# Turning the exponentials of an attention block with VectorE and DMA in place of TensorE

## The chip, the cores and the metric

The kernel runs on one core of a Trainium2 chip. The metric is the device time of one execution in microseconds. Before the change three runs took 4974.77, 4978.38 and 4980.49 us; the median is 4978.38 us.

## The reference

Four images of 32 x 32 tokens with 768 channels pass through two layers. Each layer normalizes its input by groups of channels, applies multi-head attention over the 1024 tokens of an image with relative-position biases, projects the result and adds the input again:

```python
qkv = x @ Wqkv                                    # 12 heads of 64 channels
rel_h = jnp.einsum('bhwc,hkc->bhwk', r_q, Rh)     # position biases made from q
rel_w = jnp.einsum('bhwc,wkc->bhwk', r_q, Rw)
scores = scale * q @ k.T + rel_h[..., :, None] + rel_w[..., None, :]
attn = jax.nn.softmax(scores, axis=-1)
out = (attn @ v) @ Wproj + bproj
x = x + out
```

The second layer scales q once more and adds a bias to q, k and v. Everything is in 32-bit floats.

## The kernel before

The kernel holds channels on partitions and tokens along a row. There are eight images in all (two layers of four), and each image has six pairs of heads, so 48 pairs. A pair's 1024 queries are cut into eight tiles of 128; the program calls (pair g, tile n) a unit, and a loop goes over 384 units. Units 0 to 3 of a pair are its first half of queries, units 4 to 7 the second.

What happens to a unit:

- `biases` (line 283): GpSimd adds the two position biases into an `sc` tile of 128 queries x 1024 keys, one for each of the two heads.
- `scores` (L295 to L313): TensorE multiplies q by k into a PSUM tile of two banks. VectorE adds the bias and finds the minimum of the negated sum in one instruction (L302), ACT takes the exponential with its sum (L306), VectorE inverts the sum (L310), and GpSimd scales the row (L313). The result is in `sc`, with queries on partitions.
- `transposes` (L328 to L333): the product with v needs keys on partitions. TensorE turns the 128 x 1024 tile of each head in eight blocks of 128 x 128, four to a PSUM tile `tr`. ACT copies the first four into `pt` (L331), VectorE the other four (L333). `pt` holds one half of the queries, 512, for all 1024 keys, and each head has one buffer of it.
- `weigh` (L343): after four units TensorE multiplies `pt` by v, 16 products for the two heads, which the profile counts as 32 matmuls. VectorE copies the result to `attn` (L347).

Beside this run the projections of the next pair. `project_in` (L207) makes q, k and v in groups of six products into PSUM tiles of the pool `ps_m`; `positions` (L250 to L273) makes the position products from q, copies them to a tile `t` (ACT, L255), stores them in DRAM (`tdr`, L258) and loads them back in a skewed order as `rel`, with 16 transfers of 32 partitions x 8 pieces of 128 bytes for each pair (L273). `turn_values` (L235) turns v with TensorE. `project_out` (L363, L369, L370) makes the output of the image that has ended: twelve groups, each of which loads the residual `res` (L360), adds it on VectorE and stores the sum. They are spread over the first two pairs of the next image. `load_x` and `norm_stats` fetch and measure the next image near the end of pair 4, and `norm_apply` normalizes it at the start of pair 5.

The order of TensorE's instructions is the program's own (`manual_schedule`). In each unit it is: the scores of the next unit, some groups of projections (`take`), a weighing that is due, the transposes of this unit, and turned values. The instructions of the other engines are ordered by a list scheduler, which takes whatever is ready in its own model, the earliest in the program first; once made, each engine's order is fixed, and an instruction that has to wait holds all that come behind it on its engine. All transfers are issued from SP's queue.

A half's weighing is done one unit after the half's last transposes: in unit 4 for the first half, and in unit 0 of the next pair for the second.

PSUM has eight banks: two score tiles of two banks (`ps_s`), two tiles of one bank for transposes (`ps_t`), and two for products (`ps_m`).

Of the kernel before, what the change touches and what calls it, by code (L numbers as in the profile page):

```python
# [42 lines left out]
def attention_blocks(ctx: ExitStack, tc: tile.TileContext, a: dict, out: bass.AP):  # L45
# [3 lines left out]
    const = ctx.enter_context(tc.tile_pool(name="const", bufs=1))  # L49
    wpool = ctx.enter_context(tc.tile_pool(name="weights", bufs=2))  # L50
    xpool = ctx.enter_context(tc.tile_pool(name="x", bufs=10))
    apool = ctx.enter_context(tc.tile_pool(name="attn", bufs=8))
    qkpool = ctx.enter_context(tc.tile_pool(name="qk", bufs=2))
    vtpool = ctx.enter_context(tc.tile_pool(name="vt", bufs=1))
    vpool = ctx.enter_context(tc.tile_pool(name="v", bufs=2))
    scpool = ctx.enter_context(tc.tile_pool(name="sc", bufs=6))
    ptpool = ctx.enter_context(tc.tile_pool(name="pt", bufs=2))
    tpool = ctx.enter_context(tc.tile_pool(name="t", bufs=1))
    relpool = ctx.enter_context(tc.tile_pool(name="rel", bufs=2))
    iopool = ctx.enter_context(tc.tile_pool(name="io", bufs=4))  # L60
    small = ctx.enter_context(tc.tile_pool(name="small", bufs=4))
    dram = ctx.enter_context(tc.tile_pool(name="scratch", bufs=1, space=bass.MemoryType.DRAM))
    dram2 = ctx.enter_context(tc.tile_pool(name="scratch2", bufs=2, space=bass.MemoryType.DRAM))
    ps_s = ctx.enter_context(tc.tile_pool(name="ps_s", bufs=2, space=PSUM))
    ps_t = ctx.enter_context(tc.tile_pool(name="ps_t", bufs=2, space=PSUM))
    ps_m = ctx.enter_context(tc.tile_pool(name="ps_m", bufs=2, space=PSUM))
# [17 lines left out]
    def load_w(g):  # L84
        im, pair = divmod(g, NP)
        w = wpool.tile([P, NC, 3 * P], FP, tag="w", name=f"w_{g}")
        w_of[g] = w
        nc.sync.dma_start(out=w, in_=a[f"wqkv{images[im][0]}"][pair].rearrange("p (c o) -> p c o", c=NC))

# [63 lines left out]
    def group_mean(cols, name):  # L153
        t = ps_t.tile([P, HALF], FP, tag="t", name=f"gm_{name}")
        for c in range(NC):
            nc.tensor.matmul(
                t[0:NG, 0:1], lhsT=grp[:, c, :], rhs=cols(c), start=(c == 0), stop=(c == NC - 1)
            )
        return t[0:NG, 0:1]

    def to_channels(g, name):
        t = ps_t.tile([P, HALF], FP, tag="t", name=f"gb_{name}")
        for c in range(NC):
            nc.tensor.matmul(  # L164
                t[:, c : c + 1], lhsT=grpT[:, c * P : (c + 1) * P], rhs=g, start=True, stop=True
            )
        return t[:, 0:NC]
# [27 lines left out]
    def project_in(g, which, i):  # L195

        im, pair = divmod(g, NP)
        l = images[im][0]
        xn, w = xn_of[im], w_of[g]
        cols = slice(i * HALF, (i + 1) * HALF)  # L200
        if i == 0:
            pool = vtpool if which == 2 else qkpool
            qkv_of[g, which] = pool.tile([P, S], FP, tag="qkv"[which], name=f"{'qkv'[which]}_{g}")
        to = qkv_of[g, which]
        t = ps_m.tile([P, HALF], FP, tag="m", name=f"pj_{g}_{which}_{i}")
        for c in range(NC):
            nc.tensor.matmul(  # L207
                t, lhsT=w[:, c, which * P : (which + 1) * P], rhs=xn[c][:, cols],
                start=(c == 0), stop=(c == NC - 1),
            )  # L210
            if c < NC - 1:
                yield True
# [16 lines left out]
    def turn_values(g, i):  # L229
        if i == 0:  # L230
            v_of[g] = vpool.tile([P, NT, P], FP, tag="v", name=f"v_{g}")
        t = ps_t.tile([P, 4, P], FP, tag="t", name=f"vt_{g}_{i}")
        for j in range(4):
# [4 lines left out]
    def positions(g, i):  # L238
# [7 lines left out]
        for j in range(4):  # L246
            for h in range(2):
# [5 lines left out]
                )  # L253
        t = tpool.tile([P, 2, 4, P], FP, tag="t", name=f"t_{g}_{i}")
        nc.scalar.copy(t, ps)  # L255
# [19 lines left out]

    sc_of, sps_of, pt_of, attn_of = {}, {}, {}, {}

# [36 lines left out]

    def transposes(g, n):
        half, j = divmod(n, 4)
        for h in range(2):
            if j == 0:
                pt_of[g, half, h] = ptpool.tile(
                    [P, NT, HALF], FP, tag=f"pt{h}", name=f"pt_{g}_{half}_{h}", bufs=1  # L320
                )
            pt = pt_of[g, half, h]
            sc = sc_of[g, n, h].rearrange("p y x -> p (y x)")
            for i in range(2):
                t = ps_t.tile([P, 4, P], FP, tag="t", name=f"tr_{g}_{n}_{h}_{i}")
                for k in range(4):
                    at = 4 * i + k
                    nc.tensor.transpose(t[:, k, :], sc[:, at * P : (at + 1) * P], ident)  # L328
                to = pt[:, 4 * i : 4 * i + 4, j * P : (j + 1) * P]
                if i == 0:  # L330
                    nc.scalar.copy(to, t)  # L331
                else:
                    nc.vector.tensor_copy(to, t)  # L333

    def weigh(g, half):
        im, pair = divmod(g, NP)
        if half == 0:
            attn_of[g] = apool.tile([P, S], FP, tag="attn", name=f"attn_{g}")
        av = ps_m.tile([P, HALF], FP, tag="m", name=f"av_{g}_{half}")
        for k in range(NT):  # L340
            for h in range(2):
                rows = slice(h * D, (h + 1) * D)
                nc.tensor.matmul(  # L343
                    av[rows, :], lhsT=v_of[g][:, k, rows], rhs=pt_of[g, half, h][:, k, :],
                    start=(k == 0), stop=(k == NT - 1),
                )
        nc.vector.tensor_copy(attn_of[g][:, half * HALF : (half + 1) * HALF], av)  # L347

    def project_out(im, o, i):
# [3 lines left out]
        if i == 0:  # L353
            wo_of[im, o] = wpool.tile([P, NC, P], FP, tag="wo", name=f"wo_{im}_{o}")
            nc.sync.dma_start(
                out=wo_of[im, o], in_=a[f"wo{l}"][o].rearrange("p (c o) -> p c o", c=NC)
            )
# [38 lines left out]
    with tc.manual_schedule(engines={mybir.EngineType.PE}):  # L396
# [13 lines left out]
        outs, todo = [], []  # L410
        pending = None
        for at, (g, n) in enumerate(units):
            im, pair = divmod(g, NP)
            last = pair == NP - 1
            if n == 0 and g + 1 < NPAIR:
                todo = prepare(g + 1)
            if outs and n == 1:
                todo = (
                    todo[:-4] + outs[0:2] + todo[-4:-2] + outs[2:4] + todo[-2:] + outs[4:6]
                )  # L420
                outs = outs[6:]
            if n == 6 and pair == NP - 2 and im + 1 < NI:
                load_x(im + 1)
# [8 lines left out]
            if at + 2 < len(units):  # L432
                biases(*units[at + 2])
            turn = list(late)
            late.clear()
            if not last or n > 1:
                take(todo, -(-6 * len(todo) // (NT - n)))
            if pending:
                weigh(*pending)
                if pending[1] == 1 and (pending[0] + 1) % NP == 0:  # L440
                    outs = put_out(im - 1 if pair == 0 else im)
                pending = None
            transposes(g, n)
            run(turn)
            if n == NT - 1:
                take(todo, 6 * len(todo))
                run(early)
                run(late)
            if n % 4 == 3:
                pending = (g, n // 4)  # L450
        weigh(*pending)
        outs = put_out(NI - 1)
# [48 lines left out]
```

## Time and profile before

| What | Value |
| --- | --- |
| Median of three runs | 4978.38 us |
| Profiled execution, its own time | 4976.71 us |
| Its span, first to last instruction | 4974.8 us |
| TensorE (PE) busy | 4631.3 us, 93% |
| VectorE (DVE) busy | 1874.0 us, 38% |
| ACT busy | 1587.2 us, 32% |
| GpSimd (POOL) busy | 2303.6 us, 46% |
| TensorE clock granted, mean | 0.971 |
| DMA: packets, bytes, share of 16 engines on SP's queue | 359664, 226.68 MB, 15.3% |

The page gives busy times by engine, the chain of work that ended last (followed back from the last instruction, at each step to what released it), and groups of instructions by line. In a line of a group, the name before `<-` is what is written and the names after it are what is read; then come the shape, the count, the busy time, the mean nanoseconds of one, and the idle time of the engine before them with what ended it. A chain cut to a stretch of time gives the shares of the lines in that stretch. SP's lines show the start, the length and the count of a row of DMA issues. The DMA share is the mean busy share of the 16 DMA engines.

### The profile page before, as it was taken

The page shows a single profiled execution, that of the slowest core. Times are in us where ns is not written, and L with a number is a line of the kernel's source. Part 1 is how long each engine was busy: PE and PEld are TensorE (multiplying, and loading weights), DVE is VectorE, ACT ScalarE, POOL GpSimd, SP SyncE. Part 2 cuts the span into 40 slices and gives each one's busy share as a digit, 9 for nine tenths or more (in the row PEclk, how much of TensorE's full clock was granted, in tenths as well). Part 3 has the DMA queues.
Part 4 walks back from the last instruction along what each step waited for, and adds up shares of the span by engine and source line. Part 5 has one row for each costly group of instructions (what it writes and reads, how often), then busy time and mean ns, then how long its engine had stood idle before and what let it go on. Part 6 is the DMA issues. An engine that isn't in the chain of part 4 may idle for free.

```text
span 4974.8 us, 50961 instructions
## 1 busy us (share of the span) xinstructions
PE 4631.3 (93%) x19200; PEld 2242.9 (45%) x19200; DVE 1874.0 (38%) x3328; ACT 1587.2 (32%) x2616; POOL 2303.6 (46%) x1555
## 2 busy tenths in 40 slices
PE   8999899999999999999999999999999999999998
PEld 4444444444444444444444444444444444444444
DVE  3434433334333443334433343333433334333342
ACT  2333322333223332233322333223332233322331
POOL 3555433554335543355433554335543455433552
PEclk9999999999999999999999999999999999999999
DMA  3111111111111111111011110111101111011101
GB/s 112 32 33 35 48 58 57 33 31 52 58 57 34 40 42 58 58 35 54 26 57 58 35 58 23 57 58 36 58 23 57 58 35 41 23 57 62 31 13 55
DMA packets 359908, 229.94 MB, mean 46 GB/s; under 512 B 218352, under 2 KB 316656, under 8 KB 353520
## 3 DMA queue, kind: packets, MB, share of 16 engines
q1 hardware_dynamic: 359664, 226.68, 15.3%
q8 instruction: 153, 2.51, 0.2%
q14 instruction: 91, 0.75, 0.0%
HBM read 151.10 MB, written 75.50 MB: 46 GB/s over the span
## 4 chain that ended last, share of the span: by engine, by line
PE 86%; ACT 9%; issue 3%; DMA 2%; DVE 1%; POOL 0%; SPq 0%; ACTq 0%; POOLq 0%; DVEq 0%
PE pj L207 31%; PE s L295 16%; PE av L343 14%; PE tr L328 11%; PE o L363 11%; ACT pt L331 5%; ACT t L255 2%; PE tp L250 2%; ACT sc L306 1%; PE vt L235 1%; DMA tdr<-t 1%; PE gb_rstd L164 0%; DMA xn<-in_x 0%; DVE st L150 0%; PE gb_mean L164 0%
## 5 line engine op out<-in xcount | busy, mean ns | idle before, releaser
L283 POOL TENSOR_TENSOR sc<-rel 128x1024 f32<-128x1024 f32 x768 | 1452.0, 1909 | 1069.0 <-PE tr L328 979.6
L207 PE MATMUL pj<-xn,w 128*128 128x512 f32 x3456 | 1567.1, 602 | 1.1 <-DVE xn L187 1.1
L313 POOL TENSOR_SCALAR sc<-sc,sm 128x1024 f32<-128x1024 f32 x768 | 849.5, 1118 | 1516.0 <-DVE sm L310 1509.0
L306 ACT ACTIVATE sc<-sc,sm 128x1024 f32<-128x1024 f32 x768 | 879.6, 1146 | 1140.7 <-DVE sm L302 1140.7
L302 DVE CUSTOM_DVE_ANT_0 sc<-s,sc 128x1024 f32<-128x1024 f32 x768 | 911.1, 1222 | 781.7 <-PE s L295 720.4
L207 PEld LDWEIGHTS pj<-xn,w 128*128 128x128 f32 x3456 | 634.8, 190 | 909.3 <-issue 902.6
L328 PE MATMUL tr<-ident,sc 128*128 128x128 f32 x6144 | 841.8, 281 | 211.6 <-ACT pt L331 208.1
L331 ACT COPY pt<-tr 128x512 f32<-128x512 f32 x768 | 448.3, 584 | 1761.5 <-PE tr L328 1760.0
L295 PE MATMUL s<-k,q 64*128 64x512 f32 x3072 | 900.1, 649 | 70.1 <-ACT t L255 68.6
L328 PEld LDWEIGHTS tr<-ident,sc 128*128 128x128 f32 x6144 | 683.9, 142 | 548.6 <-issue 363.5
L333 DVE COPY pt<-tr 128x512 f32<-128x512 f32 x768 | 530.1, 690 | 722.7 <-PE tr L328 717.1
L343 PE MATMUL av<-pt,v 128*64 128x512 f32 x3072 | 685.8, 599 | 0.0
L363 PE MATMUL o<-attn,wo 128*128 128x512 f32 x1152 | 534.8, 617 | 0.0
L295 PEld LDWEIGHTS s<-k,q 64*128 64x128 f32 x3072 | 304.3, 196 | 392.5 <-issue 251.7
L343 PEld LDWEIGHTS av<-pt,v 128*64 128x64 f32 x3072 | 215.3, 138 | 463.4 <-issue 441.5
L363 PEld LDWEIGHTS o<-attn,wo 128*128 128x128 f32 x1152 | 222.4, 197 | 314.3 <-issue 314.3
L347 DVE COPY attn<-av 128x512 f32<-128x512 f32 x96 | 66.4, 691 | 720.9 <-PE av L343 720.9
L310 DVE RECIPROCAL sm<-sm 128x2 f32<-128x2 f32 x384 | 63.2, 165 | 402.2 <-ACT sc L306 402.2
L369 DVE SCALAR_TENSOR_TENSOR res<-o,bo,res 128x512 f32<-128x512 f32 x96 | 72.0, 750 | 237.1 <-PE o L363 232.7
L306 ACT ACTIVATION_READ_ACCUMULATOR sc<-sc,sm 128x1 f32 x768 | 143.2, 186 | 0.0
L255 ACT COPY t<-tp 128x1024 f32<-128x1024 f32 x96 | 97.2, 1012 | 132.2 <-PE tp L250 83.6
L250 PE MATMUL tp<-tab,q 64*128 64x128 f32 x1536 | 107.8, 283 | 1.4 <-issue 0.7
(47 smaller groups left out, 772.2 us busy)
## 6 DMA issues: line engine op xcount, KB each, us to landing
w<-in_wqkv SPq DMA_DIRECT2D x48, 1152.0 KB, 5.1
tdr<-t SPq DMA_DIRECT2D x192, 256.0 KB, 2.8
rel<-tdr SPq DMA_DIRECT2D x768, 32.0 KB, 2.0
wo<-in_wo SPq DMA_DIRECT2D x48, 384.0 KB, 3.2
xn<-in_x SPq DMA_DIRECT2D x24, 512.0 KB, 6.3
res<-in_x SPq DMA_DIRECT2D x48, 256.0 KB, 2.7
mid<-res SPq DMA_DIRECT2D x48, 256.0 KB, 2.1
xn<-mid SPq DMA_DIRECT2D x24, 512.0 KB, 6.6
```

The lines of the kernel that those rows point to most:

```text
L207: nc.tensor.matmul(t, lhsT=w[:, c, which * P : (which + 1) * P], rhs=xn[c][:, cols], start=(c == 0), stop=(c == NC - 1),)
L250: nc.tensor.matmul(ps[:, h, j, :], lhsT=q[rows, at * P : (at + 1) * P], rhs=tabs[l][rows, :], start=True, stop=True,)
L283: nc.gpsimd.tensor_tensor(sc, rel[:, h, 0, n, :].unsqueeze(2).to_broadcast([P, HW, HW]), rel[:, h, 1, n, :].unsqueeze(1).to_broadcast([P, ...
L295: nc.tensor.matmul(ps[h][:, cols], lhsT=q[rows, n * P : (n + 1) * P], rhs=k[rows, cols], start=True, stop=True,)
L302: nc.vector.tensor_tensor_reduce(out=sc, in0=ps[h], in1=sc, scale=-1.0, scalar=BIG, op0=ALU.add, op1=ALU.min, accum_out=st[:, 0, h : h + 1],)
L306: nc.scalar.activation(sc, sc, AF.Exp, bias=st[:, 0, h : h + 1], scale=-1.0, accum_out=st[:, 1, h : h + 1],)
L313: nc.gpsimd.tensor_scalar(sc, sc, st[:, 2, h : h + 1], 1.0, ALU.mult, ALU.mult)
L328: nc.tensor.transpose(t[:, k, :], sc[:, at * P : (at + 1) * P], ident)
L331: nc.scalar.copy(to, t)
L333: nc.vector.tensor_copy(to, t)
L343: nc.tensor.matmul(av[rows, :], lhsT=v_of[g][:, k, rows], rhs=pt_of[g, half, h][:, k, :], start=(k == 0), stop=(k == NT - 1),)
L363: nc.tensor.matmul(t, lhsT=w[:, c, :], rhs=attn_of[im * NP + c][:, cols], start=(c == 0), stop=(c == NC - 1),)
```

## The change

The turning by TensorE goes, with the PSUM pool `ps_t` and the copies on ACT and VectorE. In its place:

- VectorE turns each head's 128 x 1024 tile in blocks of 32 x 32, one instruction for each tile and head, into a tile `tb`. Two units share one `tb`. After this a block's keys lie on the 32 partitions that held its queries, so they are not yet on the partitions of their keys.
- After every second unit SP issues 16 transfers for each head, from SBUF to SBUF. Each moves, from 32 partitions of `tb` to 32 partitions of `pt`, eight pieces of 64 floats (256 bytes) on each partition.
- `pt` holds queries in another order (quarter, block, unit, query); the copy to `attn` is made in two parts that restore it.
- The weighing of a half moves one unit later, to units 5 and 1, behind the start of the next half's turning.
- There are three score tiles in PSUM. The turned values and the small products of the normalization use the pool `ps_m`.
- Buffers in SBUF: `x` tiles 7 instead of 10, residuals (`io`) 2 instead of 4, `attn` 7 instead of 8. The projected v and the tile `t` of positions, which had buffers of their own, share the six of `sc`. The weights of a pair come as three tiles (q, k, v) of 384 KB with four buffers, instead of one of 1152 KB with two.
- The twelve output groups of an image are spread over units 2 to 7 of the next image's first pair and, from unit 0, over its second.

```diff
-    xpool = ctx.enter_context(tc.tile_pool(name="x", bufs=10))
-    apool = ctx.enter_context(tc.tile_pool(name="attn", bufs=8))
+    xpool = ctx.enter_context(tc.tile_pool(name="x", bufs=7))
+    apool = ctx.enter_context(tc.tile_pool(name="attn", bufs=7))
...
-    iopool = ctx.enter_context(tc.tile_pool(name="io", bufs=4))
+    tbpool = ctx.enter_context(tc.tile_pool(name="tb", bufs=4))
+    ptpool = ctx.enter_context(tc.tile_pool(name="pt", bufs=1))
+    iopool = ctx.enter_context(tc.tile_pool(name="io", bufs=2))
...
-    ps_s = ctx.enter_context(tc.tile_pool(name="ps_s", bufs=2, space=PSUM))
-    ps_t = ctx.enter_context(tc.tile_pool(name="ps_t", bufs=2, space=PSUM))
+    ps_s = ctx.enter_context(tc.tile_pool(name="ps_s", bufs=3, space=PSUM))
...
+    def turn(g, n):
+        half, quarter, j = n // 4, n // 2 % 2, n % 2
         for h in range(2):
+            if n % 4 == 0:
+                pt_of[g, half, h] = ptpool.tile(
+                    [P, NT, 2, 4, 2 * HW], FP, tag=f"pt{h}", name=f"pt_{g}_{half}_{h}"
+                )
             if j == 0:
-                to = pt[:, 4 * i : 4 * i + 4, j * P : (j + 1) * P]
-                if i == 0:
-                    nc.scalar.copy(to, t)
-                else:
-                    nc.vector.tensor_copy(to, t)
+                tb_of[h] = tbpool.tile([P, HW, 2, HW], FP, tag="tb", name=f"tb_{g}_{n}_{h}")
+            tb, pt = tb_of[h], pt_of[g, half, h]
+            nc.vector.transpose(tb[:, :, j, :], sc_of[g, n, h])
+            if j == 1:
+                for y in range(4):
+                    for r in range(4):
+                        nc.sync.dma_start(
+                            out=pt[32 * y : 32 * y + 32, :, quarter, r, :],
+                            in_=tb[32 * r : 32 * r + 32, y::4, :, :].rearrange("p k n i -> p k (n i)"),
+                        )
...
-            if pending:
-                weigh(*pending)
...
-            transposes(g, n)
-            run(turn)
+            if n % 4 == 1 and at > 4:
+                weigh(*(units[at - 2][0], n // 4 ^ 1))
+                if n == 1 and pair == 0:
+                    outs = put_out(im - 1)
+            run(ready)
```

In the new loop `turn(g, n)` stands ahead of the projections of the unit.

## The prediction

> **What bounds the kernel now.** I read the page's shares first, then the chain that ended last, then the chain over single stages, then the groups, and last SP's queue, which the change loads. The chain by engine and by line:
>
> ```profile
> PE 86%; ACT 9%; issue 3%; DMA 2%; DVE 1%; POOL 0%; SPq 0%; ACTq 0%; POOLq 0%; DVEq 0%
> PE pj L207 31%; PE s L295 16%; PE av L343 14%; PE tr L328 11%; PE o L363 11%; ACT pt L331 5%; ACT t L255 2%; PE tp L250 2%; ACT sc L306 1%; PE vt L235 1%; DMA tdr<-t 1%; PE gb_rstd L164 0%; DMA xn<-in_x 0%; DVE st L150 0%; PE gb_mean L164 0%
> ```
>
> TensorE is the bound. The transposes hold it directly (tr, 11%) and a second time through the copy that it waits for (pt, 5%). One unit of the chain in order of time (start, duration, what) shows how:
>
> ```profile
> 2778.76 1.92 PE s L295 x8
> 2780.67 3.63 PE pj L207 x8
> 2784.30 0.45 PE tr L328 x4
> 2784.76 0.02 issue
> 2784.78 0.59 ACT pt L331
> 2785.37 0.14 issue
> 2785.51 1.11 PE tr L328 x8
> 2786.62 1.92 PE s L295 x8
> ```
>
> From 2784.30 to 2786.62, 2.3 us of each unit, TensorE serves the turning of the exponentials. The groups that the change removes, and the row by which I price its new VectorE work:
>
> ```profile
> L302 DVE CUSTOM_DVE_ANT_0 sc<-s,sc 128x1024 f32<-128x1024 f32 x768 | 911.1, 1222 | 781.7 <-PE s L295 720.4
> L328 PE MATMUL tr<-ident,sc 128*128 128x128 f32 x6144 | 841.8, 281 | 211.6 <-ACT pt L331 208.1
> L331 ACT COPY pt<-tr 128x512 f32<-128x512 f32 x768 | 448.3, 584 | 1761.5 <-PE tr L328 1760.0
> L333 DVE COPY pt<-tr 128x512 f32<-128x512 f32 x768 | 530.1, 690 | 722.7 <-PE tr L328 717.1
> ```
>
> Stages differ, so I cut one image (2475.9 to 3093.7 us, 617.8 us) at its weighings. The chain by line of a pair with output projections (2475.9 to 2598.8), then of the two halves of a pair without (2721.7 to 2769.2 and 2769.2 to 2811.7):
>
> ```profile
> by line: PE o L363 26.8%; PE pj L207 26.1%; PE s L295 14.0%; PE av L343 11.4%; PE tr L328 9.6%; ACT pt L331 4.8%; DMA tdr<-t 2.3%; ACT t L255 1.7%; issue 1.4%; PE vt L235 1.1%; PE tp L250 0.9%; SPq L258 0.3%; ACTq L255 0.0%; ACTq L331 0.0%
> ...
> by line: PE pj L207 40.5%; PE s L295 16.4%; PE av L343 14.8%; PE tr L328 13.4%; ACT pt L331 5.0%; PE tp L250 4.7%; ACT t L255 4.3%; issue 1.7%; ACTq L255 0.1%; ACTq L331 0.0%
> ...
> by line: PE pj L207 32.7%; PE s L295 18.8%; PE av L343 16.5%; PE tr L328 14.7%; ACT pt L331 6.7%; issue 4.4%; PE vt L235 3.8%; ACT sc L306 2.9%; DVE sc L302 0.2%; DVE sm L302 0.2%; ACTq L331 0.0%; DVEq L302 0.0%
> ```
>
> **What comes off TensorE.** Without tr, pt, their issue time, the wait for the copy of t and the landing of tdr, the pair with outputs falls from 122.9 to about 98.6 us (9.6, 4.8, 1.7, 2.3 and 1.4% taken off). The halves without outputs fall from 47.5 to 35.9 us (13.4, 5.0, 4.3 and 1.7% off) and from 42.5 to 32.5 us (14.7 and 6.7% off, and 1 us of issue). I take the waits for t as gone: t gets one of six buffers in place of one, and with three score tiles in PSUM a score no longer needs the tile that ACT is copying. If both stay, the pair costs 2 to 5 us more.
>
> **What is added, and where it queues.** VectorE gets 768 block transposes of 128x1024. The trace has none. From below, the nearest 1024-column row is the normalization at L187 (808 ns); from above, twice L302 (2.44 us); I take L302's 1.22 us, f32 at the same width. 768 x 1.22 = 937 us against 530 us of copies removed: VectorE goes from 1874 to about 2290 us, half of any likely span. The attention copy in two halves of 256 columns adds some 10 us of its 66. None of it is on the path while VectorE is half idle; at 2.44 us it would be near 3230 us, still under the span, but the last transposes of a half would come later. ACT loses 448 us.
>
> SP gets 48 pairs x 4 x 2 x 16 = 6144 transfers of 32 partitions x 8 pieces of 256 bytes (64 KB). Nothing in the trace moves SBUF to SBUF. The nearest row is rel<-tdr, also 32 partitions x 8 pieces, in bursts of 16; first SP's queue, then the page's row with the time to landing:
>
> ```profile
> 990.58 8.94 SPq L273 DMA_DIRECT2D rel<-tdr  x16
> ...
> 1082.72 7.84 SPq L273 DMA_DIRECT2D rel<-tdr  x16
> ```
>
> ```profile
> rel<-tdr SPq DMA_DIRECT2D x768, 32.0 KB, 2.0
> ```
>
> Many bursts take 7.72 us: 0.48 us for each transfer, 0.56 in the dear bursts. A lone load or store issues in 0.33 us; xn loads go at 0.68 (three in 2.04). Ends 0.33 and 0.68; I take 0.48, that of the same shape. 6144 x 0.48 = 2960 us of SP: it fits the span in total. The DMA engines are at 15%; while a rel burst runs their share is 0.37 to 0.48, so pieces of twice the bytes make at most 0.96, still under the rate of issue, but narrowly. So the cost is not a sum but a loop.
>
> **The loop.** Each head has one pt buffer. The first 32 transfers of a half (issued from unit 1 or 5) overwrite what the weighing in that same unit reads, so they start when it ends; 32 more follow (unit 3 or 7); the next weighing needs the last landing. From weighing end to last landing: 64 x 0.4825 = 30.9 us, plus 1.5 us (2.0 to landing less the last issue) = 32.4. The weighing takes 7.0 (32 matmuls, 7.02 us in the chain). The loop is 39.4 us a half, whatever TensorE does. The first half also has four tdr (median 0.38) and two w issues (0.36) in SP's queue, with some 0.04 us between instructions: 2.4 us; the second has one w, 0.4. The sixteen rel issues, 7.7 us, I put at nothing: they wait for tdr's landing, so they come behind the second 32, while SP has 8.5 us of landing and weighing with no pt transfer to issue. If they come in front, each first half pays 7.7.
>
> TensorE's own halves, 35.9 and 32.5 us, are shorter than the loop, so it idles before the weighing: 39.4 + 2.4 - 35.9 = 5.9 us, and 39.8 - 32.5 = 7.3. What such a pause costs next, by stage (us, busy and count of each engine, granted clock, DMA share, GB/s):
>
> ```profile
> 3120.00:3124.00 4.00, 0.75 (x4) 0.32 (x4) 0.00 (x0) 1.01 (x1) 0.00 (x0) 0.88 0.42 131
> 3124.00:3128.00 4.00, 4.00 (x7) 1.35 (x6) 1.62 (x3) 0.82 (x1) 0.00 (x0) 0.50 0.47 135
> 3128.00:3132.00 4.00, 4.00 (x8) 1.62 (x7) 1.66 (x4) 1.67 (x4) 0.46 (x1) 0.77 0.38 59
> ```
>
> After a pause of 3.25 us TensorE works about 6 us at a granted clock of one half, which loses some 2.9 us, and here the weighing itself runs in it. Halves: 39.4 + 2.4 + 2.9 = 44.7 and 39.4 + 0.4 + 2.9 = 42.7, a pair 87.4 us where 90.0 were. Nearly all that TensorE gains there goes to the loop. The Trainium skill ("TensorE: Matmul & The Clock Gate", Part 1: The HAM clock gate) has the same sign: half rate after an idle window of about 3.4 us.
>
> A rule of the skill speaks against the change: "DMA: Bandwidth & Descriptors", Rules for kernel authors, wants small transfers coalesced, since under 64 KB one pays mostly overhead; its table gives 0.95 us for 64 KB. Were these serial, a half would be an estimated 64 x 0.95 + 9 = 70 us and the kernel near 6900. The rel bursts, each landing 2.0 us after an issue 0.48 us behind the last, overlap, so the row decides.
>
> **Smaller buffers.** x tiles go from 10 to 7: five tiles of the next image instead of two are loaded only when the old ones are released, at the end of pair 4, in SP's queue behind up to 15 us of pt issues, and the normalization waits for all. That half had 50.1 us with a 4.87 us wait on xn. Bounds: 43.7 (as before, turning gone) to 65 (15 us of queue, cold clock); I take 55. The residual's buffers go from 4 to 2: a load waits for the landing of the store two before it, behind a burst of 15 us. VectorE is in order, so a late residual holds it, and with it the scores and the evacuations. Outputs come about 13 us apart (one in each of the four units of a 52 us half), so two of them cover most: 0 to 20 us a pair, taken as 4, and 1.4 where the loop shows.
>
> **Sum.** An image: two pairs with outputs at 104, two at 87.4, pair 4 at 44.7 + 55, pair 5 at 87.7: 570 us against 617.8, less 47.6, seven times: 333. The first image, without outputs, gains about 20; the last weighing now waits for 32 issues and a landing, about 20 lost. The profiled execution (span 4974.8, time 4976.7, 1.7 under the median of 4978.4) falls to a span of 4642, so about 4645.
>
> **Rivals.** (1) The transfers are hidden. At 0.33 us a half's loop is 64 x 0.33 + 1.5 + 7.0 = 29.6, under TensorE's halves. Then only the tr, pt and t chains go: about 490 us an image, 4050 in all. For: lone issues take 0.33. Against: every issue in a row took more. (2) rel comes in front of the second 32, or SP blocks on a transfer whose wait ends later: 7.7 to 10 us on the first half of pairs 2 to 5, 31 to 40 an image, 4860 to 4940. For: rel now goes out 13 us after the first tdr (1069.27 to 1082.72), which could fall ahead of the second 32. Against: those need only VectorE, ready earlier. (3) Slower: issue of the new transfers. The gain of 333 us is spread over about 8 loop-bound halves an image; 5 us a half takes it back, 0.08 us a transfer: from 0.56 us on, the dear rel burst, the kernel is not faster. At 0.68 the loop is 43.5 + 8.5 = 52 us, 55 with the clock, in all twelve halves: about 680 an image, 5450. For: two 256-byte sides on 32 partitions, unmeasured. Against: rel's 0.48, in the same shape.
>
> **How the numbers follow.** Forecast 0.50 (4500 to 4800), hidden 0.12, queue 0.13, slower issue 0.25. Of the forecast, 0.01 falls within 0.2% of 4978 (10 us, about what a measurement tells from no change) and 0.02 above; of the queue case 0.02 and 0.02. Faster 0.47 + 0.12 + 0.09 = 0.68, same 0.03, slower 0.25 + 0.04 = 0.29. The range goes from 4350, half way to hidden, to 5150, an issue of about 0.60; about 0.1 is left out at each end. The likeliest case's own range is 4500 to 4800.
>
> **What would show it.** No tr or pt copies; pt<-tb x6144 on SP at 0.48 us, landing 2 us; VectorE's transposes at 1.2 us; av waiting for DMA some 6 us in pairs 2 to 5, not in pairs 0 and 1; clock below 0.97. It is wrong if the issue period is another, if av starts without waiting, or if TensorE waits longer at the norms or outputs than I gave.

## The result, and the profile after the change

The changed kernel takes 6078.85 us (median of four runs, 6076.74 to 6082.63) against 4977.52 us before: a ratio of 1.2213, with an interval of 1.2192 to 1.2234. It is 22% slower where the forecast said 7% faster. The profiled execution took 6077.1 us, its span is 6075.4 us, and TensorE's mean granted clock fell from 0.971 to 0.814.

The busy times on the page, and the chain that ended last by engine and by line:

```profile
PE 4051.5 (67%) x13056; PEld 1654.8 (27%) x13056; DVE 2266.8 (37%) x3424; ACT 1141.9 (19%) x1848; POOL 2301.8 (38%) x1555
...
SPq 30%; PE 22%; DMA 5%; issue 3%; DVE 2%; POOL 1%; ACT 1%; DVEq 0%; ACTq 0%
SPq L338 27%; PE av L350 8%; PE pj L210 5%; PE o L376 4%; PE s L298 3%; SPq L276 3%; DMA pt<-tb 2%; DMA tdr<-t 2%; DVE tb L334 1%; PE tp L253 1%; DMA xn<-mid 1%; ACT sc L309 1%; DMA res<-mid 0%; POOL sc L286 0%; SPq L261 0%
```

SP's queue was at 0% of the chain and is now its largest part, nearly all of it L338, the new transfers. TensorE, 93% busy before, is at 67%. (The followed chain accounts for some two thirds of the span; the rest is not attributed.) The groups that wait for the transfers:

```profile
L350 PE MATMUL av<-pt,v 128*64 128x512 f32 x3072 | 982.2, 734 | 1583.2 <-DMA pt<-tb 1470.7
...
L334 DVE STREAM_TRANSPOSE tb<-sc 128x1024 f32<-128x1024 f32 x768 | 923.4, 1229 | 1674.9 <-DMA pt<-tb 1444.7
```

The weighing (`av`) sits idle for 1470.7 us until transfers land, and VectorE's transposes for 1444.7 us until a `tb` has been read. The view of one tile, `tb`, gives the price (min/median/max in ns) and the landing, and SP's own waits close the loop (total us, times, longest):

```profile
L338 SPq DMA_DIRECT2D pt<-tb x6144: 585/609/1958, 75.9 to 5997.9; - x199
DMA to landing us min/median/max: 2.1/2.1/9.8
```

```profile
SPq L338 <- PE av L350: 751.5, 89, 11.1
```

An issue holds SP for 0.609 us. SP's queue over some stretches (start, length, what, count) shows the period, and where the transfers of `rel` stand:

```profile
1648.58 20.85 SPq L338 DMA_DIRECT2D pt<-tb  x32
...
2583.78 0.90 SPq L338 DMA_DIRECT2D pt<-tb  x1
2586.82 7.73 SPq L276 DMA_DIRECT2D rel<-tdr  x16
2594.60 73.78 SPq L338 DMA_DIRECT2D pt<-tb  x95
```

32 transfers in 20.85 us are 0.652 us each, 0.61 of issue and 0.04 between instructions. `rel`, 32 partitions x 8 pieces too, but of half the bytes and read from DRAM, still goes at 7.73 / 16 = 0.483. And `rel` comes after the first of a second 32, in front of the other 31: the long row is those 31, a wait for the weighing, and the next 64. Last, while such a burst runs (us, busy and count of PE, PEld, DVE, ACT and POOL, granted clock, DMA share, GB/s):

```profile
1626.00:1647.00 21.00, 21.00 (x64) 9.05 (x60) 9.71 (x17) 5.33 (x9) 7.44 (x6) 1.00 0.38 92
1900.00:1921.00 21.00, 7.18 (x14) 2.30 (x14) 8.34 (x10) 2.85 (x5) 9.74 (x6) 0.71 0.41 99
```

The DMA engines are at 0.41, so they are not what limits a burst. The second row is a pair without outputs: TensorE has 7 us of work in 21 and its clock falls to 0.71; the first is a pair with outputs, where TensorE has work beside the burst.

Halves from weighing end to weighing end, in the image that begins at 1548.5 us (pairs 0 and 1 carry the outputs; us, predicted in brackets):

| Pair | First half | Second half | Pair |
| --- | --- | --- | --- |
| 0 | 78.2 | 63.9 | 142 (104) |
| 1 | 67.0 | 56.2 | 123 (104) |
| 2 | 66.4 | 53.2 | 120 (87.4) |
| 3 | 66.0 | 51.6 | 118 (87.4) |
| 4 | 67.2 | 54.6 | 122 (99.7) |
| 5 | 65.9 | 53.8 | 120 (87.7) |

This image takes 744 us; it took 617.8 before, and 570 were predicted. The first image, which has no outputs and was to gain about 20 us, takes 800.6 us to the end of its last weighing instead of 622.7.

### The profile page after: what moved, and what is told of

Its sections match the earlier page's. It is cut to its first block, busy times and chain, and to the rows that moved or that the text cites. A ratio compares the mean times of both kernels' runs of the same rounds, so it can differ in the third digit from the quotient of the medians.

```text
span 6075.4 us, 45766 instructions
## 1 busy us (share of the span) xinstructions
PE 4051.5 (67%) x13056; PEld 1654.8 (27%) x13056; DVE 2266.8 (37%) x3424; ACT 1141.9 (19%) x1848; POOL 2301.8 (38%) x1555
## 4 chain that ended last, share of the span: by engine, by line
SPq 30%; PE 22%; DMA 5%; issue 3%; DVE 2%; POOL 1%; ACT 1%; DVEq 0%; ACTq 0%
SPq L338 27%; PE av L350 8%; PE pj L210 5%; PE o L376 4%; PE s L298 3%; SPq L276 3%; DMA pt<-tb 2%; DMA tdr<-t 2%; DVE tb L334 1%; PE tp L253 1%; DMA xn<-mid 1%; ACT sc L309 1%; DMA res<-mid 0%; POOL sc L286 0%; SPq L261 0%
## 5 line engine op out<-in xcount | busy, mean ns | idle before, releaser
L350 PE MATMUL av<-pt,v 128*64 128x512 f32 x3072 | 982.2, 734 | 1583.2 <-DMA pt<-tb 1470.7
L210 PE MATMUL pj<-xn,w 128*128 128x512 f32 x3456 | 1604.8, 613 | 192.9 <-DVE res L382 191.8
L334 DVE STREAM_TRANSPOSE tb<-sc 128x1024 f32<-128x1024 f32 x768 | 923.4, 1229 | 1674.9 <-DMA pt<-tb 1444.7
L350 PEld LDWEIGHTS av<-pt,v 128*64 128x64 f32 x3072 | 323.2, 168 | 2238.6 <-issue 1898.3
L298 PE MATMUL s<-k,q 64*128 64x512 f32 x3072 | 790.7, 620 | 12.0 <-DVE sm L305 12.0
L298 PEld LDWEIGHTS s<-k,q 64*128 64x128 f32 x3072 | 281.7, 190 | 385.1 <-issue 300.7
L357 DVE COPY attn<-av 128x256 f32<-128x256 f32 x192 | 72.2, 418 | 781.2 <-PE av L350 781.2
L253 PEld LDWEIGHTS tp<-tab,q 64*128 64x128 f32 x1536 | 93.2, 187 | 85.2 <-issue 45.8
L159 PE MATMUL gm_mean<-mv,grp 128*32 128x1 f32 x96 | 12.5, 199 | 154.0 <-DVE mv L154 154.0
L239 ACT COPY v<-vt 128x512 f32<-128x512 f32 x96 | 55.6, 580 | 160.1 <-PE vt L238 159.8
```

Of the source, the lines that this page charges most:

```text
L210: nc.tensor.matmul(t, lhsT=w[:, c, :], rhs=xn[c][:, cols], start=(c == 0), stop=(c == NC - 1),)
L253: nc.tensor.matmul(ps[:, h, j, :], lhsT=q[rows, at * P : (at + 1) * P], rhs=tabs[l][rows, :], start=True, stop=True,)
L298: nc.tensor.matmul(ps[h][:, cols], lhsT=q[rows, n * P : (n + 1) * P], rhs=k[rows, cols], start=True, stop=True,)
L334: nc.vector.transpose(tb[:, :, j, :], sc_of[g, n, h])
L350: nc.tensor.matmul(av[rows, :], lhsT=v_of[g][:, k, rows], rhs=pt_of[g, half, h][:, k].rearrange("p q r t -> p (q r t)"), start=(k == 0), s ...
```

## The experiments

The theory after the result: a transfer from SBUF to SBUF has a fixed price of issue on its queue, 0.65 us, and the single `pt` buffers put 64 of them in series with each half's weighing. The first rival: the transfers themselves (bytes or pieces through the DMA engines) set the time, and SP only shows it. The second: it is what stands around the transfers, the place of `rel`, the smaller buffers, or an engine held in its order.

**Forms of transfer, measured by themselves.** Behind all the work, 16 issues of each of eight forms are put in a row:

```diff
+        for y, r in slots:   # 512 B pieces; the others: 128 B, 4 pieces, one piece of 2 KB, ...
+            nc.sync.dma_start(out=pt[32 * y : 32 * y + 32, :, r, :], in_=wide[32 * r : 32 * r + 32, :, 0:P])
...
+        for y, r in slots:   # 256 B pieces read from DRAM
+            nc.sync.dma_start(out=pt[32 * y : 32 * y + 32, :, 0, r, :], in_=src[:, 0:8, :])
```

> The changed kernel with eight rows of 16 extra transfers behind its work, one form to a line: L480 the form of pt (32 partitions x 8 pieces of 256 bytes), L483 pieces of 128 bytes, L486 4 pieces, L490 pieces of 512 bytes, L493 one piece of 2 KB, L496 pt's form with its 8 pieces side by side in the destination, L501 pt's form read from DRAM, L504 pt's form from ACT's queue. They tell what makes the issue 0.61 us where the rel transfers take 0.45. If it is the number of pieces: L486 about 0.4, L493 about 0.35, the others 0.6. If it is bytes: L483 0.5, L490 above 0.7. If it is two scattered sides in SBUF: L496 near 0.45 and L501 near 0.45, whatever the bytes. If it is a fixed price of a transfer within SBUF: all but L501 at 0.6. The time is that of the changed kernel plus some 100 us.

The kernel took 6135.81 us in one run, 57 us more than the changed kernel. Measured, line by line (issue in ns, min/median/max): the change's own form, pieces of half the bytes, half as many pieces, pieces of 512 B, one piece of 2 KB, a contiguous destination, a source in DRAM, and the own form on ACT's queue:

```profile
L480 SPq DMA_DIRECT2D forms<-forms_src x16: 585/592/619, 6016.7 to 6052.6; - x16
L483 SPq DMA_DIRECT2D forms<-forms_src x16: 585/609/633, 6057.1 to 6073.8; - x16
L486 SPq DMA_DIRECT2D forms<-forms_src x16: 586/600/609, 6074.5 to 6085.4; - x16
L490 SPq DMA_DIRECT2D forms<-forms_src x16: 606/616/624, 6086.1 to 6095.9; - x16
L493 SPq DMA_DIRECT2D forms<-forms_src x16: 588/589/615, 6096.6 to 6106.1; - x16
L496 SPq DMA_DIRECT2D forms<-forms_src x16: 608/609/642, 6106.8 to 6116.6; - x16
L501 SPq DMA_DIRECT2D forms<-tdr x16: 302/431/614, 6117.2 to 6126.9; - x16
L504 ACTq DMA_DIRECT2D forms<-forms_src x16: 592/622/717, 6118.9 to 6130.6; - x16
```

With both sides in SBUF the issue takes 0.59 to 0.62 us (medians) on either queue, for 32 KB as for 128 KB and for one piece as for eight. With the source in DRAM it takes 0.30 to 0.61, median 0.43. The whole row with the DRAM source is no shorter than the others (6117.2 to 6126.9): it ran beside the row on ACT's queue, and its later transfers waited for earlier ones to land. After such a wait an issue took 0.30 us there, but still 0.59 to 0.63 in ACT's row, with both sides in SBUF. So the price of an issue hangs on where the two sides lie and is paid per transfer. The row by which I had priced it, `rel`, has a DRAM side; it is the one that shows the shorter period in a row by itself, 0.483.

**Half the transfers on ACT's queue.**

```diff
-                        nc.sync.dma_start(
+                        (nc.sync, nc.scalar)[r % 2].dma_start(
```

> The changed kernel with half of the pt transfers (r odd) issued from ACT's queue instead of SP's; all else as it was. Theory (the issue of 64 transfers a half on one queue, 0.65 us each, sets a loop of 42 us of issue, a landing and a weighing): a burst of 32 takes about half of its 20.9 us, the loop of a half falls from some 53 to 32 us, and with the halves of TensorE (33 to 56 us) the time falls to between 4200 and 4800 us. Rival (the transfers themselves, DMA engines or SBUF ports, are what is slow): each queue then issues at half the pace, a burst of 32 still takes some 20 us, and the time stays at 5900 to 6080. Second rival (ACT held by its issues delays the exponentials): bursts shorten, but the time stays above 5000.

Measured: 5167.08 us, ratio 1.0387 (1.0370 to 1.0404), 912 us less than the changed kernel, but outside the 4200 to 4800. ACT's queue, then ACT's waits and one of SP's, then the DMA share in such a burst (last but one column):

```profile
2235.86 12.80 ACTq L338 DMA_DIRECT2D pt<-tb  x16
2253.91 12.74 ACTq L338 DMA_DIRECT2D pt<-tb  x16
```

```profile
ACT sc L309 <- DMA pt<-tb: 1743.9, 103, 27.3
ACT t L258 <- DMA pt<-tb: 953.5, 45, 23.7
```

```profile
SPq L338 <- DMA pt<-tb: 305.0, 1091, 1.9
```

```profile
2254.00:2266.00 12.00, 5.19 (x16) 1.66 (x14) 5.70 (x8) 0.00 (x0) 9.71 (x6) 0.89 1.06 151
```

A burst of 32 falls from 20.9 to 12.8 us, so the first rival is refuted for the changed kernel: the same bytes move faster when two queues issue them. It does not halve to 10.4, because the DMA engines now seem full (share 1.06, where one queue drove them to 0.41): a transfer lands 3.1 us after its issue at the median, where it was 2.1, and SP's issues wait 305.0 us for earlier transfers. At most eight transfers are in flight (one for each completion semaphore, see the next run), and how much of the limit is theirs is not separated. The kernel gains less than the bursts, as the second rival of this run had it: ACT, which issues in its own order, keeps the exponentials waiting behind transfers. The Trainium skill ("DMA: Bandwidth & Descriptors", Issuing engines are not separate DMA queues) says that issuing from several engines saves only the sequencer's time to issue, "which is usually small relative to the DMA itself". The first part is what this run shows. The second doesn't hold for such a burst: of its 20.9 us issue was the whole, and 8 us of it came off.

**The position transfers (`tdr`, `rel`) on ACT's queue**, so that SP has only the `pt` bursts.

```diff
-            nc.sync.dma_start(
+            nc.scalar.dma_start(
                 out=td[h, i * HALF : (i + 1) * HALF, :].rearrange("(j p) r -> p j r", p=P),
...
-                        nc.sync.dma_start(out=rel_of[g][32 * y : 32 * y + 32, h, ax, :, :], in_=src)
+                        nc.scalar.dma_start(out=rel_of[g][32 * y : 32 * y + 32, h, ax, :, :], in_=src)
```

> The changed kernel with the tdr and rel transfers issued from ACT's queue. Theory: in the first half of each pair rel's 16 issues and the wait for tdr stand between the pt issues and hold them by some 10 us; taken out, the first halves of pairs 2 to 5 fall from 66 to about 56 us and the time by 250 to 480 us, to 5600 to 5830. Rival (they only fill time in which SP would wait anyway): the time changes by less than 60 us.

Measured: 6004.16 us in one run, 75 us less, between the two expectations. The first halves of pairs 2 to 4 fell from 66 to 68 us only to 62, and that of pair 1 rose from 67 to 81. The first burst of a half, and a wait that SP did not have before:

```profile
2528.70 30.70 SPq L338 DMA_DIRECT2D pt<-tb  x32
```

```profile
SPq L338 <- DMA rel<-tdr: 423.3, 253, 12.7
```

The burst still takes 30.7 us though nothing else stands in SP's queue: its transfers now wait for those of `rel`, with which they share no tile. What they share are the program's completion semaphores, which tell that a transfer has landed: the trace shows eight, handed out in turn to the transfers of both queues, so a transfer waits until the one that had its semaphore has landed. That `rel` in front of a burst costs what it did in SP's queue is therefore not separated here; the wait only moved. The semaphores' part was not tried by itself.

**The smaller buffers alone**, in the kernel before:

```diff
-    xpool = ctx.enter_context(tc.tile_pool(name="x", bufs=10))
-    apool = ctx.enter_context(tc.tile_pool(name="attn", bufs=8))
+    xpool = ctx.enter_context(tc.tile_pool(name="x", bufs=7))
+    apool = ctx.enter_context(tc.tile_pool(name="attn", bufs=7))
...
-    iopool = ctx.enter_context(tc.tile_pool(name="io", bufs=4))
+    iopool = ctx.enter_context(tc.tile_pool(name="io", bufs=2))
```

> The kernel before the change with the smaller buffers alone: x tiles 7 in place of 10, residuals 2 in place of 4, attn 7 in place of 8; TensorE still turns the exponentials. The prediction's terms for them: pair 4's second half longer by 5 us or so an image (it was 50.1 us, 55 taken), outputs 4 us a pair longer, so 5 + 2 x 4 = 13 us an image, 7 images: about 90 us, 5070 us. Rival (SyncE's queue is free of the new transfers, and so the loads are hidden): within 20 us of before. Rival (the buffers are a main part of the loss): over 5200 us.

Measured: 5007.42 us, ratio 1.0062 (1.0047 to 1.0077): 30 us more, between the first two expectations and a third of the 90. The view of the tile `xn`, which the projections and the norm read, has a wait on the residuals (us, times) that the kernel before does not show:

```profile
  DVE res L369: 36.3, 14
```

So the buffers are 30 of the 1101 us, as far as they act without the bursts.

**The count of transfers at equal bytes.** Two kernels have the changed kernel's structure with block buffers over four units (two `tb` of 16 KB a partition for four of 8 KB). They differ only in that one moves a piece of 512 B where the other moves two of 256 B in two transfers: 32 or 64 transfers a half, issued together after the fourth unit (`j` now counts the units of a half). The copy to `attn` is in one part.

```diff
-                    [P, NT, 2, 4, 2 * HW], FP, tag=f"pt{h}", name=f"pt_{g}_{half}_{h}"
+                    [P, NT, 4, 4 * HW], FP, tag=f"pt{h}", name=f"pt_{g}_{half}_{h}"
...
-                tb_of[h] = tbpool.tile([P, HW, 2, HW], FP, tag="tb", name=f"tb_{g}_{n}_{h}")
+                tb_of[h] = tbpool.tile([P, HW, 4, HW], FP, tag="tb", name=f"tb_{g}_{n}_{h}")
...
-            if j == 1:
+            if j == 3:
                 for y in range(4):
                     for r in range(4):
...
+                        for q in range(2):
+                            nc.sync.dma_start(
+                                out=pt[32 * y : 32 * y + 32, :, r, 64 * q : 64 * q + 64],
+                                in_=tb[32 * r : 32 * r + 32, y::4, 2 * q : 2 * q + 2, :].rearrange(
+                                    "p k n i -> p k (n i)"
+                                ),
+                            )
```

> The changed kernel with block buffers over four units in place of two (two of 16 KB for four of 8 KB, the same space); the 64 transfers of a half stay as they are, 32 a head of 256 B pieces, but are issued together after the fourth unit. It is the control for the next kernel. Theory (a transfer costs its fixed issue, 0.65 us, and the loop over the single buffers adds it up): a half is 64 x 0.653 = 41.8 us of issue, 2.1 us to land, and then four units of two reductions and two transposes on VectorE, 4 x 4.9 = 20 us, before the next burst may begin: about 64 us, against a mean of 59.5 now, so 6100 to 6700 us. Rival (the loop is broken up by the later burst and the transfers run beside the other work): 5000 to 5800 us.

```diff
-                        for q in range(2):
-                            nc.sync.dma_start(
-                                out=pt[32 * y : 32 * y + 32, :, r, 64 * q : 64 * q + 64],
...
+                        nc.sync.dma_start(
+                            out=pt[32 * y : 32 * y + 32, :, r, :],
+                            in_=tb[32 * r : 32 * r + 32, y::4, :, :].rearrange("p k n i -> p k (n i)"),
+                        )
```

> As the kernel with the buffers over four units, but each transfer carries all four units, 8 pieces of 512 B a row: the same bytes with half as many transfers, 32 in place of 64 a half, at the same places. Theory (count times a fixed price): 32 x 0.653 = 20.9 us less in each of 96 halves, 2006 us, as far as other work does not become the bound; 1400 to 2000 us below the control, 4600 to 5200 us. Rival (the bytes that move through the 16 DMA engines set the time, since these are the same): within 3% of the control. Half-way (price grows with the piece): 500 to 1000 us below.

Measured: with 64 transfers 6468.31 us, ratio 1.2991 (1.2972 to 1.3011), in the expected range. With 32 transfers 5102.79 us, ratio 1.0249 (1.0233 to 1.0264): 1366 us less, just short of the 1400. The tile view of the first and then of the second:

```profile
L338 SPq DMA_DIRECT2D pt<-tb x6144: 585/608/1847, 76.0 to 6389.6; - x199
DMA to landing us min/median/max: 2.1/2.1/6.9
```

```profile
L337 SPq DMA_DIRECT2D pt<-tb x3072: 585/616/1720, 91.5 to 5021.0; - x192
...
DMA to landing us min/median/max: 2.4/4.3/7.5
```

The weighing's wait for the transfers, in the first and in the second:

```profile
PE av L352 <- DMA pt<-tb: 1860.1, 129, 25.5
```

```profile
PE av L349 <- DMA pt<-tb: 703.5, 86, 20.8
```

A transfer of 128 KB is issued in the time of one of 64 KB. Half the count takes 14.2 us off each of 96 halves (1366 / 96), of the 20.9 that issue alone would give; the weighing's wait falls by 1157 us. Some 2 us of the missing 6.7 are the later landing. The others are not separated: they may be halves in which TensorE's own work is now as long as the loop. This is the clearest test of the theory: bytes, tiles and order are the same, and the count differs. The pieces differ too, 256 B against 512 B, but the forms showed the same issue for both, and in a burst of the first kernel the DMA share is 0.42, so that the pieces do not limit it. In a burst of the second kernel the next limit shows (a window of each):

```profile
2610.00:2630.00 20.00, 7.93 (x22) 2.89 (x20) 6.33 (x9) 3.25 (x6) 10.10 (x7) 0.80 0.42 100
```

```profile
2626.00:2644.00 18.00, 18.00 (x54) 7.61 (x52) 5.84 (x11) 5.33 (x9) 6.29 (x5) 1.00 1.01 189
```

At 128 KB every 0.66 us the DMA share is 1.01: the engines are about full, at 189 GB/s in this view where the changed kernel's burst had 99. The skill's rule for many small transfers (the same page, Rules for kernel authors), to coalesce them, is what this pair of kernels shows, 1366 us for it; the page puts its bound under 64 KB, and here it paid from 64 KB to 128 KB.

**These 32 transfers on two queues.** The kernel with 512 B pieces, with every second transfer on ACT's queue:

```diff
-                        nc.sync.dma_start(
+                        (nc.sync, nc.scalar)[r % 2].dma_start(
                             out=pt[32 * y : 32 * y + 32, :, r, :],
```

> Both heads by transfers of 512 B pieces (5102.8 us), with every second transfer on ScalarE's queue. Theory (what holds that kernel is still SyncE's issue, 26% of its chain, 20.9 us a half): 10.5 us on each queue, and as ScalarE is busy 22% it can carry 10.5 us a half: 4400 to 4800 us. Rival (ScalarE is held behind transfers that wait, as with 256 B pieces on two queues, 5167 us): 4900 to 5200 us.

Measured: 5234.5 us, ratio 1.0516 (1.0499 to 1.0534), 132 us more than on one queue and above both ranges. SP's share of a burst, and the last 12 of the 16 on ACT's queue beside it (the first 4 begin at 2571.53):

```profile
2571.52 18.52 SPq L337 DMA_DIRECT2D pt<-tb  x16
```

```profile
2577.12 15.01 ACTq L337 DMA_DIRECT2D pt<-tb  x12
```

The 32 transfers take 20.6 us, from 2571.5 to 2592.1, where one queue takes about 21; the quickest burst of this kernel takes 19.9 us, of the other 21.1. The engines were full already, so the second queue buys about 1 us a half. What costs the 132 us is probably the ACT order that it disturbs (`v` and the exponentials wait 1284 us for transfers on ACT, 666.2 and 617.8); no run separates it. The theory's premise, that issue still held that kernel, failed: with 512 B pieces issue and DMA engines end nearly together.

**One head by each way.** Head 0 is turned by TensorE as before the change, with both copies on ACT; head 1 by VectorE and the transfers, 32 a half, with two `pt` buffers. PSUM is divided as before the change.

```diff
-        for h in range(2):
...
+        tb, pt = tb_of[1], pt_of[g, half, 1]
+        nc.vector.transpose(tb[:, :, j, :], sc_of[g, n, 1])
...
+    def transposes(g, n):
+        half, j = divmod(n, 4)
+        if j == 0:
+            pt_of[g, half, 0] = ptpool.tile([P, NT, HALF], FP, tag="pt0", name=f"pt_{g}_{half}_0")
...
+                nc.tensor.transpose(t[:, k, :], sc[:, at * P : (at + 1) * P], ident)
+            nc.scalar.copy(pt[:, 4 * i : 4 * i + 4, j * P : (j + 1) * P], t)
```

> Head 0 is turned by TensorE as in the kernel before (both copies on ACT), head 1 by VectorE and transfers as in the changed kernel, with two pt buffers for head 1. SP has 32 transfers a half, 21 us, under TensorE's halves, and no loop through one buffer. Theory: TensorE is the bound again, with half of its turning gone: between 4450 and 4750 us, faster than both. Rival (the cost lies in the buffers, the late weighing and the order, not in the number of transfers): above 5200.

Measured: 4810.74 us, ratio 0.9666 (0.9652 to 0.9680): faster than both kernels, though 61 us outside the range. Then the same with 512 B pieces, 16 transfers a half, and one `pt` buffer for each head:

```diff
-        if j == 1:
+        if j == 3:
...
-                        out=pt[32 * y : 32 * y + 32, :, quarter, r, :],
+                        out=pt[32 * y : 32 * y + 32, :, r, :],
```

> The kernel with head 0 by TensorE and head 1 by transfers (4810.7 us), with head 1's block buffer over four units: 16 transfers of 512 B pieces a half in place of 32 of 256 B, and one buffer of weights for head 1 in place of two. Theory (what is left of the transfers' price is still on the path, SyncE's queue 9% of its chain, 433 us): 4450 to 4750 us. Rival (the issue is hidden in that kernel, and its bound is the order of ScalarE's copies behind the late weighing): 4780 to 4900 us.

Measured: 4648.49 us, ratio 0.9337 (0.9323 to 0.9351), 162 us less, in the range and the fastest kernel here. Piece, count and buffer changed together, so this run does not say which gave how much. The chain by engine, of the first and of the second:

```profile
PE 65%; POOL 9%; SPq 9%; ACT 6%; DVE 5%; issue 4%; DMA 3%; ACTq 0%; POOLq 0%; DVEq 0%
```

```profile
PE 4278.0 (92%) x16128; PEld 1955.5 (42%) x16128; DVE 1891.6 (41%) x3040; ACT 1545.2 (33%) x2616; POOL 2306.1 (50%) x1555
...
PE 67%; POOL 8%; SPq 6%; DVE 6%; ACT 6%; issue 4%; DMA 3%; ACTq 0%; POOLq 0%; DVEq 0%
```

TensorE is the bound again, at 92% and a granted clock of 0.965, with half of its transposes gone (410 us of them are left, 842 before).

**Two orders of that kernel.** Its ACT copies wait 895.5 us for the weighing that still reads head 0's buffer. First the transposes of a half's first unit are put behind that weighing; then, instead, the weighing is put one unit earlier.

```diff
-            transposes(g, n)
+            if n % 4 == 1:
+                transposes(g, n - 1)
+            if n % 4:
+                transposes(g, n)
```

> As the kernel before it, but the TensorE transposes of a half's first unit are put after the weighing that still reads head 0's buffer (at the second unit), so that ScalarE's copies no longer wait at the head of its queue for that weighing (970.8 us of idle time ahead of them in the kernel with 32 transfers). Theory: that wait held the exponentials and with them the next units; it falls below 300 us and the time by 100 to 400 us against the kernel before it. Rival (ScalarE had spare time there; the wait is only the place where its idle time shows): within 1%.

```diff
-            if n % 4 == 1 and at > 4:
-                weigh(*(units[at - 2][0], n // 4 ^ 1))
+            if n % 4 == 0 and at > 0:
+                weigh(*(units[at - 1][0], n // 4 ^ 1))
```

> The best kernel so far (head 0 by TensorE, head 1 by transfers of 512 B pieces, 4648.5 us) with the weighing one unit earlier, as the kernel before the change has it. Theory (ScalarE's copies wait 895.5 us for the late weighing, and this now ends at its cause): the burst of 16 takes 10.5 us and lands 3.4 us later, 14 us, against one to one and a half units of 12 us until the weighing, so the wait for the transfers stays below 300 us in all; 4500 to 4620 us. Rival (that wait was spare time of ScalarE, and TensorE is the bound at 92%): within 1%. Rival (the weighing now waits for the transfers): 4700 to 4900 us, with the wait of av for pt above 400 us.

Measured: 4748.38 us, ratio 0.9536 (0.9520 to 0.9552), and 4925.27 us, ratio 0.9896 (0.9881 to 0.9911): 100 and 277 us more than without. The waits of the kernel without, of the first and of the second order:

```profile
ACT pt L345 <- PE av L355: 895.5, 95, 15.1
POOL sc L287 <- PE tr L344: 515.8, 116, 11.2
PE av L355 <- DMA pt<-tb: 145.0, 28, 12.5
```

```profile
ACT pt L345 <- PE tr L344: 1518.5, 355, 20.1
POOL sc L287 <- PE tr L344: 808.6, 115, 18.1
```

```profile
ACT pt L345 <- PE tr L344: 1970.2, 340, 23.4
PE av L355 <- DMA pt<-tb: 386.0, 51, 12.5
```

The first order missed both of its expectations, and ACT's wait got another name and grew: by these two runs that wait was spare time. In the first order the `sc` buffers come free later, and GpSimd's biases wait 808.6 us for the transposes, not 515.8. In the second the weighing waits 386.0 us for transfers, not 145.0. It missed its theory; the rival that the weighing waits for the transfers comes nearest, but the time is 25 us over its range and the wait 14 us under its bound of 400. TensorE's idle time rose from 371 us to 425 and to 588. So here the weighing two units late is worth its buffer: it keeps the transfers' price off TensorE's path.

## Why the prediction was wrong, step by step

- **"I take 0.48, that of the same shape" is the step that failed.** The period is 0.652 us, near the upper of the two ends given (0.33 and 0.68). The shape was the same, but `rel` reads from DRAM and the new transfers have both sides in SBUF; the forms measured in rows put 0.43 against 0.59 to 0.62 of issue, whatever the pieces. The periods differ by 0.17 us, which is 64 x 0.17 = 10.9 us a half.
- **The loop's formula was right.** With 0.652 in it, 64 x 0.652 + 1.5 + 7.0 = 50.2, and with 0.4 of other issue and 2.9 of cold clock a second half is 53.5 us. Measured in pairs 2, 3 and 5: 51.6 to 53.8. The cut from 64 to 32 transfers in the two controlled kernels supports it. That the single `pt` buffers make the series was not tried by itself; it rests on this fit and on the waits (SP 751.5 us for the weighing, the weighing 1470.7 us for the transfers).
- **"The sixteen rel issues, 7.7 us, I put at nothing" also failed.** Behind the first of the second 32 they lengthen that burst from 20.9 to 30.7 us (1838.8 to 1869.5, for one), 9.8 us, which the second rival had priced (7.7 to 10). I argued from when the data are ready; but SP's order is fixed beforehand, by the scheduler's model, and one early transfer of the second 32 does not let the others pass. A first half is then 50.2 + 2.4 + 2.9 + 9.8 = 65.3; measured 65.9 to 67.2.
- **Together these two account for pairs 2 to 5**: seven halves (all but pair 4's second) x 10.9 plus four x 9.8 are 115.5 us; measured 479 against 362 predicted, 116.5 more. Moving `rel` to the other queue did not bring its part back, so this second term rests on the lengths of the bursts and not on a run.
- **Pairs 0 and 1 at 104.** TensorE was taken as their limit. The loop, 65 + 53.5 = 119 us, is longer, and pair 1 measures 123. Pair 0 takes 142, 23 more than the loop. Two things make it. The residuals' loads stand behind a burst in SP's queue, and TensorE waits for VectorE's output (stretch 1615 to 1690):

```profile
PE av L350 <- DVE res L382: 15.7, 1, 15.7
PE pj L210 <- DVE res L382: 12.4, 1, 12.4
```

  Of the first wait only the last 3 us count, since until about 1614 the weighing's own transfers had not landed. The second, with the projections behind it, puts off the next weighing by some 12 us. That is the mechanism named ("a late residual holds it"), put at 4 us of 0 to 20. The buffers without the bursts cost only 30 us in all. The other 8 us are in SP's queue: in the first half a load of weights waits for the projections to free its buffer, and `rel` and the other 31 stand behind it (stretch 1547 to 1695):

```profile
SPq L91 <- PE pj L210: 7.2, 1, 7.2
```

  The second rival has this case ("SP blocks on a transfer whose wait ends later"), and the forecast put it at nothing.
- **Pair 4's second half at 55: right in size**, 54.6 here and 56 to 59 in the other images that load a next one. But the loop alone now gives 53.5, so the agreement is in part luck and does not test the reason I gave, the late loads of `x`.
- **VectorE: right.** Transposes of 1.229 us on average (1.22 taken), 2266.8 us in all (2290). TensorE's removed time came off too, but off the path.
- **The DMA engines "narrowly" under the rate of issue: right as far as the runs go.** At 0.652 a burst drives them to 0.41. With two queues they are about full (1.06) at one transfer every 0.40 us (12.8 / 32), so 0.48 would still have been the slower of the two; no run issues at that rate.
- **The clock: right in direction** (below 0.97), larger in size. TensorE's busy time is 4051.5 us where 4631.3 - 841.8 = 3789.5 were left: 262 us more for the same work at a mean clock of 0.814. The weighings alone go from 685.8 to 982.2 us. The 2.9 us taken for a half come out about right (96 halves of 2.9 are 278), but I had counted seven halves of an image and not all twelve.
- **The outcome was the third rival**, "slower: issue of the new transfers", with its point of decision at 0.56 us and its row at 0.68, against which I had set "rel's 0.48, in the same shape". Its 5450 us falls short of 6079 mainly because it left out `rel`'s place and what pair 0 adds.

## What to carry to other kernels

Price a transfer's issue from a row with the same two sides, not only the same shape, and where the trace has none, let the dearest lone row weigh as much as the nearest one. Count transfers and not bytes as long as the DMA share of a burst is well under 1; from there on a second queue buys little. When a unit is replaced as the bound, move only as much work as the new path carries beside the old: with pieces of 256 B half of the turning gained 3.3% and all of it cost 22%, with 512 B half gained 6.6% and all cost 2.5%.

## What the runs showed of the hardware that I had not expected

- An issue with both sides in SBUF takes 0.59 to 0.62 us, on SP's and on ACT's queue, for 32 to 128 KB and for one to eight pieces on a partition; with a source in DRAM it is 0.30 to 0.61, 0.43 at the median.
- Bursts of 256 B pieces fill the 16 DMA engines at 64 KB every 0.40 us (two queues, share 1.06), those of 512 B pieces at 128 KB every 0.66 us (one queue, share 1.01), which is 1.2 times the bytes in the same time. A second queue brought the latter only to 0.64.
- A burst on one queue at 64 KB every 0.65 us leaves the DMA share at 0.41, though each transfer takes 2.1 us to land.
